# A residual sum moved from VectorE to TensorE and ScalarE, and two more buffers for scanned pairs, in the first state-space layer of a four-layer network

## The chip, the cores and the metric

The kernel runs on one core of one Trainium2 chip. A core has TensorE (matrix products, results into PSUM), VectorE, ScalarE and GpSimd for work on tiles, and a sync engine that issues most of the DMAs. The profile calls them PE (with PEld for the weight loads), DVE, ACT, POOL and SP. Each engine takes its instructions in the order in which the program lists them, and waits on semaphores for the others. The metric is the time of one execution on the device in microseconds (us), the median of several runs.

## The reference, cut to what matters

The input is `x` of 8 samples, 384 channels, 32 x 32 pixels, all in fp32. Four layers follow each other, each with a residual: `x = x + layer(group_norm(x))`. Layer 0 is a state-space layer (Mamba), layer 1 a deformable convolution, layer 2 a second state-space layer with a layer norm and an MLP, layer 3 a shift with a small convolution. The change touches layer 0 alone, where the 1024 pixels of a sample are a sequence:

```python
xz = xseq @ in_proj_w.T                 # 384 -> 2 x 768 channels
xin, z = jnp.split(xz, 2, axis=-1)
u = silu(causal_conv3(xin) + conv_b)
dt, Bm, Cm = split(u @ x_proj_w.T)      # 24, 16 and 16 wide
dt = softplus(dt @ dt_proj_w.T + dt_proj_b)
# for each token, 768 channels x 16 states:
h = exp(dt * A) * h + (dt * u) * Bm     # the scan
y = sum over the states of h * Cm, plus u * D
out = (y * silu(z)) @ out_proj_w.T      # 768 -> 384 channels
x = x + out                             # the residual
```

## The kernel before, in words

**Tiling.** In layer 0 a *step* is one half (512 tokens) of one sample, so there are 16 steps; even steps are first halves, odd ones second halves, which take the state over from the first. The 768 inner channels are 6 blocks `j` of 128 partitions, the 16 states are 8 pairs `m`. One *unit* is one `(j, m)`: a tile of 128 partitions x (2 states x 512 tokens). A step has 48 units, t = 0 to 47.

**One unit.** ScalarE writes the decays `da` into PSUM (`decays`, L437, two instructions, two buffers). GpSimd writes `db` (`inputs`, L442, three buffers). VectorE scans (`scan`, L452) and multiplies by C (`with_c`, L466) into a tile `hs`. In 3 or 4 units of every 16 GpSimd does that product instead (L463), and then the scan itself writes into `hs`. TensorE sums the pairs into the PSUM tile `y` by products with the identity (`read_out`, L483). The tiles `hs` have four buffers; one is free again when its two `read_out` products are done. A unit's `read_out` is put one to three units later than its scan. After the eight pairs of a block, VectorE multiplies `y` by the gate (`close`, L503, in slot 1, 9, 17, ... of the step); `y` has a single buffer.

**The order of everything else.** The engines' order is written out by hand. `plan` makes four lists of slots (`act`, `dve`, `pool`, `pe`), one slot per unit, and the loop over the units empties a slot of each as it goes. The slots hold work on three steps at once: the current one, the next one (`nxt`: norm, input projection `inner` L333 in slots 15, 16, 17, 24, 25, 26, convolution, `x_proj`, `dt_proj`) and the previous one (`prev`: its output projection). Within a unit `act` comes first, then the scan, `with_c`, `keep_last` (even steps: ScalarE saves the last state, L458), the decays of unit t + 2, then `dve`, `pool` and `pe`.

**The output projection.** `out_proj` (L516) sums, for each of three blocks `o` of output channels, six products `wout x u` of the previous step into a PSUM tile, three products in slot 8 and three in slot 9 (then 10 and 11, 12 and 13). `out_take` (L536, slots 11, 13 and 15 of `dve`) adds the tile to the residual tile `x` on VectorE and writes it there; after the third block one DMA stores it (L527). `x` was loaded by `residual` (L508). All PSUM tiles of projections share three buffers (tag `mm`), the `dt_proj` tile (L389, slots 6, 14, ...) among them. After the last step the three blocks follow each other without other work between them.

**Waits that matter below.** `soft_exp` (L395 to L398, `act`, slot 15 for one of the blocks) waits for `dt_proj` of slot 14; `conv_last` (L337, `act`, slot 16) waits for `inner` of slot 15; `close` in slot 17 waits for the `read_out` products of the eight pairs before it.

Of the kernel before, what the change touches and what calls it, by code (L numbers as in the profile page):

```python
# [8 lines left out]
F32 = mybir.dt.float32  # L9
AF = mybir.ActivationFunctionType  # L10
ALU = mybir.AluOpType
# [4 lines left out]
P = 128  # L16
# [6 lines left out]
ND = DI // P  # L23
# [3 lines left out]
TS = L // 2  # L27
# [64 lines left out]
class Net:  # L92
# [107 lines left out]
    def ssm_layer(self, li, src, dst, shift=None):  # L200
        tc, nc, ins = self.tc, self.nc, self.ins
        mlp = li == 2
        gp_c, gp_add = GP_C[li], GP_ADD[li]
        with ExitStack() as ctx:
            wp = ctx.enter_context(tc.tile_pool(name=f"w{li}", bufs=1))
            p1 = ctx.enter_context(tc.tile_pool(name=f"p1_{li}", bufs=1))
            p2 = ctx.enter_context(tc.tile_pool(name=f"p2_{li}", bufs=2))
# [5 lines left out]
            for h in (1, 0):  # L213
                x = p2.tile([P, G, TS], F32, name="x", tag="x")
# [44 lines left out]
            def w_mid(src, k):  # L259
                t = p2.tile([P, k, W_MID // k], F32, name="wm", tag="wm", bufs=3)  # L260
                n = src.shape[2]
                nc.sync.dma_start(out=t[:, :, :n], in_=src)
                return t
# [180 lines left out]
            def scan(s, j, m):  # L444
                if j == 0 and m == 0 and s["h"] == 0:
                    s["sib"]["st"] = p2.tile([P, ND, NS], F32, name="st")
                da, db = s["da", m], s["db", m]
                h = da
                if m in gp_c[s["h"]][j % 2]:
                    h = s["hs", m] = p2.tile([P, 2, TS], F32, name="hs", tag="hs", bufs=4)  # L450
                h1, da1, db1 = (t.rearrange("p i l -> p (i l)") for t in (h, da, db))
                nc.vector.tensor_tensor_scan(h1, da1, db1, 0.0, ALU.mult, ALU.add)  # L452
                s["h", m] = h
# [6 lines left out]
            def with_c(s, j, m):  # L460
                c = s["bc"][m][:, 1]
                if m in gp_c[s["h"]][j % 2]:
                    nc.gpsimd.tensor_tensor(s["hs", m], s["hs", m], c, ALU.mult)  # L463
                else:
                    hs = s["hs", m] = p2.tile([P, 2, TS], F32, name="hs", tag="hs", bufs=4)
                    nc.vector.tensor_tensor(hs, s["da", m], c, ALU.mult)  # L466

            def add_pair(s, j, m):
# [41 lines left out]
            def out_proj(s, o, k0, k1):  # L510
                if k0 == 0:
                    wo = w_mid(wout_d[:, :, o * P : (o + 1) * P], ND) if mlp else wout[:, :, o * P : (o + 1) * P]
                    s["out", o] = self.psum("ps_o"), wo
                ps, wo = s["out", o]
                for k in range(k0, k1):
                    nc.tensor.matmul(ps, wo[:, k, :P], s["u"][:, k, :], start=(k == 0), stop=(k == ND - 1))  # L516

            def store(s, o):
                if mlp:
# [9 lines left out]
            def out_take(s, o):  # L529
                if mlp:  # L530
                    if o == 0:
                        s["t"] = p2.tile([P, G, TS], F32, name="t", tag="xn", bufs=3)
                    nc.scalar.copy(s["t"][:, o, :], s["out", o][0])
                else:
                    xo = s["x"][:, o, :]
                    nc.vector.tensor_tensor(xo, xo, s["out", o][0], ALU.add)  # L536
                    store(s, o)

            def mlp_up(s, q, f):
# [51 lines left out]
            def plan(prev, s, nxt):  # L591
                act, dve, pool, pe = queues = [[[] for _ in range(T + NU)] for _ in range(4)]

                def put(q, t, fn, *args):
                    if not args or args[0]:
                        q[t].append((fn, *args))

                for j in range(ND):
                    t = NU * j
                    put(dve, t + 1, close, *((s, j - 1) if j else (prev, ND - 1)))  # L600
                    put(pe, (0, 9, 18, 27, 33, 41)[j], z_proj, s, j)
                    g = (3, 11, 20, 29, 35, 44)[j]
                    put(act, g, gate, s, j)
                    if j in (2, 3):
                        put(act, g, silu, nxt, 3 * (j - 2), 3 * (j - 1))
                    put(act, g, exp_ln)

                    n, k = (s, j + 2) if j + 2 < ND else (nxt, j + 2 - ND)
                    put(pe, t + 6, dt_proj, n, k)
                    put(act, t + 7, soft_exp, n, k)  # L610
                    put(dve, t + 8, soft_rest, n, k)
                    put(act, t + 9, soft_ln, n, k)
                    put(pool, t + 10, soft_sum, n, k)
                put(pe, 0, norm_load, nxt)
                if nxt and nxt["h"] == 0:
                    put(dve, 2, norm_stats, nxt, 0)
                    put(dve, 3, norm_stats, nxt, 1)
                    put(dve, 3, lambda n: n.update(gn_mv=self.gn_aggr(n["gn_st"])), nxt)
                    put(pe, 4, lambda n: n.update(gn_ps=self.gn_mean(n["gn_mv"])), nxt)
                    put(dve, 5, lambda n: n.update(gn_grp=self.gn_dev(n["gn_mv"], n["gn_ps"])), nxt)  # L620
                    put(act, 6, lambda n: n.update(gn_dm=self.gn_square(n["gn_grp"][1])), nxt)
                    put(pe, 6, lambda n: n.update(gn_ps=self.gn_mean2(n["gn_dm"])), nxt)
                    put(dve, 7, lambda n: n.update(gn_var=self.gn_sum(n["gn_grp"][0], n["gn_ps"])), nxt)
                    put(act, 8, lambda n: n.update(gn=self.gn_rstd(n["gn_grp"][0], n["gn_var"])), nxt)
                    put(act, 8, lambda n: n["sib"].update(gn=n["gn"]), nxt)
                put(act, 9, norm_apply, nxt)
                if mlp:
                    put(pe, 10, ln_mean, nxt)
                    put(dve, 11, ln_center, nxt)
                    put(act, 12, ln_square, nxt)  # L630
                    put(pe, 12, ln_var, nxt)
                    put(act, 13, ln_rstd, nxt)
                    put(dve, 13, ln_scale, nxt)
                    put(act, 14, ln_affine, nxt)
                for d, t in enumerate((15, 16, 17, 24, 25, 26)):
                    put(pe, t, inner, nxt, d)
                    put(act, t + 1, conv_last, nxt, d)
                    put(dve, t + 2, conv, nxt, d)
                put(pe, 30, x_proj, nxt, 0, ND // 2)
                put(pe, 31, x_proj, nxt, ND // 2, ND)  # L640
                put(act, 32, x_store, nxt)
                for m in range(NU):
                    put(pool, 41 + m, load_bc, nxt, m)
                put(act, 7 if mlp else 9, residual, prev)
                for o, (t, e) in enumerate(((1, 2), (3, 4), (5, 6)) if mlp else ((8, 9), (10, 11), (12, 13))):
                    put(pe, t, out_proj, prev, o, 0, ND // 2)
                    put(pe, e, out_proj, prev, o, ND // 2, ND)
                    put(act if mlp else dve, e + (1 if mlp else 2), out_take, prev, o)
                if mlp:
                    ups = ((7, 8, 11, 13), (22, 23, 28, 29), (37, 38, 39, 40))  # L650
                    downs = ((19, 20, 21), (34, 35, 36), (43, 44, 45))
                    for q, g in enumerate((17, 33, 42)):
                        for f, t in enumerate(ups[q]):
                            put(pe, t, mlp_up, prev, q, f)
                            put(act, t + 1, up_take, prev, q, f)
                        put(act, g, gelu, prev)
                        put(act, g, exp_ln)
                        for o, t in enumerate(downs[q]):
                            put(pe, t, mlp_down, prev, q, o)
                            put(dve, t + 2, down_take, prev, q, o)  # L660
                return queues
# [6 lines left out]
            with tc.manual_schedule(engines=ENGINES):  # L668
                s = steps[0]
# [34 lines left out]
                for i, (s, j, m) in enumerate(units):  # L704
                    c, t = divmod(i, T)
                    if t == 0:
# [6 lines left out]
                        act, dve, pool, pe = queues  # L713
                        over = [q[T:] for q in queues]
                    mine = m in gp_c[s["h"]][j % 2]
                    for r in early.pop(i, ()):
                        read_out(*units[r])
                    run(act[t])
                    scan(s, j, m)
                    if not mine:  # L720
                        with_c(s, j, m)
# [14 lines left out]
                    if mine:  # L736
                        with_c(s, j, m)
# [6 lines left out]
                    k = 3 if mine else 2 if m in gp_add else 1  # L744
# [12 lines left out]
                    stats = list(range(last))  # L757
                for o in range(G):
                    out_proj(s, o, 0, ND)
                    out_take(s, o)  # L760
                if mlp:
                    kernels_a()
# [1084 lines left out]
```

## Time and profile before

| what | value |
|---|---|
| time, median of 3 runs (lowest, highest) | 9474.54 us (9471.22, 9475.02) |
| the profiled execution: time, span | 9480.32 us, 9478.5 us |
| mean granted TensorE clock of that execution | 0.948 |
| layer 0 within the span | about 60 to 3041 us |
| its steps, from first scan to first scan | first 177.4 us; then even ones 182 to 183, odd ones 188 to 192 |
| a scan / a product with C on VectorE | 2290 / 1225 ns |
| the residual add L536, 48 times | 677 ns |

A line of instruction groups gives the source line, engine, operation and tiles (out<-in), then the count, the busy time, the mean of one, and the idle time of the engine just before. Each fp32 matrix product is recorded as two MATMUL instructions, called passes here; so the 16 x 3 x 6 = 288 products of `out_proj` show as 576. In a timeline a line is a run of like instructions: start, length, engine, source line, and in brackets the engine's idle time before it with what ended it.

### The profile page before, as it was taken

To read this page: it belongs to the slowest core of one execution; us is meant where nothing else is said; L and a number is where in the kernel's file an instruction comes from. 1 tells how busy PE (TensorE), PEld (TensorE's weight loads), DVE (VectorE), ACT (ScalarE), POOL (GpSimd) and SP (SyncE) were. 2 spreads that over 40 slices of the span, in tenths; PEclk is the share of its full clock that TensorE was granted. 3 is DMA by queue.
4 is the path that set the end of the run, shared out by engine and by line. 5 is a ranking of instruction groups with operands and counts; after the bars stand their busy time and mean duration, and the time that the engine had idled before them with its cause. 6 is when DMAs were issued, how large, how long until landed. Compare 5 with 4: busy or idle time off the path is not lost. (4 is left out here: it accounts for less than half of the span.)

```text
span 9478.5 us, 87409 instructions
## 1 busy us (share of the span) xinstructions
PE 8496.4 (90%) x27916; PEld 4511.6 (48%) x27916; DVE 8121.2 (86%) x8881; ACT 6479.3 (68%) x10147; POOL 5774.0 (61%) x3801
## 2 busy tenths in 40 slices
PE   7898888889887899999999997699999999999987
PEld 3333333333333677677777776244343443434333
DVE  7999999999997678778778777899999999999973
ACT  6666666666664677778778777667777777777750
POOL 7888888888887000000000000899999999999974
PEclk8999999999998999999999998799999999999998
DMA  2111211121111233333333333233232433333336
GB/s 92 68 56 46 85 53 53 50 85 56 49 68 51 77 80 88 90 83 84 93 79 88 89 83 87 92 100 95 91 94 87 121 112 96 93 91 90 120 102 127
DMA packets 566065, 791.98 MB, mean 84 GB/s; under 512 B 244243, under 2 KB 397235, under 8 KB 542041
## 3 DMA queue, kind: packets, MB, share of 16 engines
q1 hardware_dynamic: 503492, 775.85, 27.9%
q10 hardware_dynamic: 62100, 10.44, 0.7%
q8 instruction: 223, 3.65, 0.2%
q14 instruction: 250, 2.04, 0.1%
HBM read 716.49 MB, written 69.66 MB: 83 GB/s over the span
## 5 line engine op out<-in xcount | busy, mean ns | idle before, releaser
L442 POOL TENSOR_TENSOR db<-du,bc 128x1024 f32<-128x1024 f32 x1536 | 3611.1, 2356 | 419.0 <-DVE hs L452 230.7
L452 DVE TENSOR_TENSOR_SCAN da<-da,db 128x1024 f32<-128x1024 f32 x1272 | 2912.7, 2290 | 199.4 <-ACT da L437 145.4
L483 PE MATMUL y<-hs,ident 128*128 128x512 f32 x5184 | 2605.0, 638 | 376.2 <-DVE hs L466 233.8
L437 ACT ACTIVATE da<-dt,na 128x512 f32<-128x512 f32 x3072 | 2120.0, 691 | 911.1 <-DVE hs L466 679.9
L410 POOL TENSOR_TENSOR dt<-dt,sp_e 128x512 f32<-128x512 f32 x192 | 244.2, 1272 | 2932.1 <-DVE sp_e L402 2932.1
L483 PEld LDWEIGHTS y<-hs,ident 128*128 128x128 f32 x5184 | 1018.0, 203 | 1863.2 <-issue 1125.3
L1515 PE MATMUL wacc<-fsm,fxk 128*128 128x221 f32 (+34 forms) x10624 | 1657.1, 315 | 98.1 <-DVE fsm L1485 95.5
L1515 PEld LDWEIGHTS wacc<-fsm,fxk 128*128 128x128 f32 x10624 | 1570.1, 195 | 236.5 <-DVE fsm L1485 159.5
L466 DVE TENSOR_TENSOR hs<-da,bc 128x1024 f32<-128x1024 f32 x1272 | 1557.7, 1225 | 115.5 <-PE y L483 12.1
L1485 DVE TENSOR_TENSOR fsm<-fhy,fhx 128x170 f32<-128x170 f32 (+42 forms) x3216 | 1170.8, 428 | 346.2 <-PE wacc L1515 319.3
L1445 ACT ACTIVATE fhy<-fpyx,cell 128x416 f32<-128x416 f32 (+9 forms) x1280 | 645.5, 576 | 388.7 <-DVE fsm L1485 388.7
L1468 DVE TENSOR_TENSOR fxk<-fxt,fwk 128x1024 f32<-128x1024 f32 (+1 forms) x688 | 787.2, 1180 | 10.3 <-ACT fxt L1247 10.3
L452 DVE TENSOR_TENSOR_SCAN hs<-da,db 128x1024 f32<-128x1024 f32 x264 | 602.4, 2282 | 70.4 <-POOL db L430 29.4
L463 POOL TENSOR_TENSOR hs<-hs,bc 128x1024 f32<-128x1024 f32 x264 | 622.3, 2357 | 35.8 <-ACT st L458 35.3
L470 POOL TENSOR_TENSOR hs<-hs 128x512 f32<-128x512 f32 x480 | 609.5, 1270 | 3.5 <-DVE hs L466 3.5
L566 PE MATMUL ps_m<-hid,wm 128*128 128x512 f32 x1152 | 535.9, 610 | 29.7 <-ACT hid L559 24.2
L544 PE MATMUL ps_h<-t,wm 128*128 128x512 f32 x1152 | 539.1, 606 | 16.0 <-DVE x L573 15.8
L1450 ACT ACTIVATE fhy<-fhy,cols 128x1344 f32<-128x1344 f32 (+10 forms) x368 | 530.7, 1442 | 12.0
L458 ACT COPY st<-da 128x2 f32<-128x2 f32 x624 | 97.9, 157 | 505.4 <-DVE hs L466 503.9
L1156 PE MATMUL ps_off<-fxn,fow 128*98 128x465 f32 (+10 forms) x896 | 386.6, 579 | 0.0
L1432 ACT ACTIVATE fhx<-fpyx,cell 128x544 f32<-128x544 f32 (+8 forms) x640 | 380.0, 666 | 0.0
L566 PEld LDWEIGHTS ps_m<-hid,wm 128*128 128x128 f32 x1152 | 220.5, 194 | 329.8 <-issue 261.4
(203 smaller groups left out, 9870.2 us busy)
## 6 DMA issues: line engine op xcount, KB each, us to landing
bc<-bcd SPq DMA_DIRECT2D x256, 1024.0 KB
fpyx<-fposd SPq DMA_DIRECT2D x640, 256.0 KB
wm<-in_w SPq DMA_DIRECT2D x96, 768.0 KB
x<-x SPq DMA_DIRECT2D x71, 768.0 KB
winr<-in_win SPq DMA_DIRECT2D x192, 192.0 KB
x<-in_x SPq DMA_DIRECT2D x40, 768.0 KB
fpyx<-fposd SPq DMA_DIRECT2D x24, 1024.0 KB
wm<-in_wout SPq DMA_DIRECT2D x48, 384.0 KB
```

Of the source, the lines that this page charges most:

```text
L437: nc.scalar.activation(da[:, i, :], s["dt", j], AF.Exp, scale=na[:, j, n : n + 1])
L442: nc.gpsimd.tensor_tensor(db, du, s["bc"][m][:, 0], ALU.mult)
L452: nc.vector.tensor_tensor_scan(h1, da1, db1, 0.0, ALU.mult, ALU.add)
L463: nc.gpsimd.tensor_tensor(s["hs", m], s["hs", m], c, ALU.mult)
L466: nc.vector.tensor_tensor(hs, s["da", m], c, ALU.mult)
L470: nc.gpsimd.tensor_tensor(hs[:, 0, :], hs[:, 0, :], hs[:, 1, :], ALU.add)
L483: nc.tensor.matmul(s["y"], self.ident, s["hs", m][:, i, :], start=first and i == 0, stop=k == NU - 1 and i == n - 1,)
L566: nc.tensor.matmul(ps, s["w2"][:, f, o * P : (o + 1) * P], s["hid", q][:, f, :], start=(f == 0), stop=(f == 3))
L1445: nc.scalar.activation(hy[:, at : at + (yb - ya) * W], pyx[:, 0, ya * W : yb * W], AF.Abs, bias=bias)
L1468: nc.vector.tensor_tensor(t[:, :n], x, wk[:, j : j + 1, :].to_broadcast([P, n, P]), ALU.mult)
L1485: nc.vector.tensor_tensor(self.sub(sm, at, [(r * w, n), (w, r), (1, w)]), self.sub(hy, hy_at[by] + xa, [(r * W, n), (W, r), (1, w)]), self ...
L1515: nc.tensor.matmul(a[:, ya - 4 * o : yb - 4 * o, xa:xb], k, self.sub(sm, sm_at[by], [(w, yb - ya), (1, w)]), start=False, stop=False,)
```

## The change

`hs` gets six buffers in layer 0 (four in layer 2, as before). The residual is no longer added by VectorE: a seventh product, the identity times the residual tile, goes into the same PSUM sum (`add_residual`, in `pe` slots 10, 12 and 14; in slot 14 it stands behind `dt_proj`), and ScalarE copies the sum from PSUM to the tile `x`, in `act` slots 11, 13 and 15 (in slot 15 behind `soft_exp`). The stop flag of the sum moves to the added product. The same is done for the three blocks after the last step. Layer 2 keeps its order and its operations.

```diff
+        nhs = 4 if mlp else 6
...
-                    h = s["hs", m] = p2.tile([P, 2, TS], F32, name="hs", tag="hs", bufs=4)
+                    h = s["hs", m] = p2.tile([P, 2, TS], F32, name="hs", tag="hs", bufs=nhs)
...
-                    hs = s["hs", m] = p2.tile([P, 2, TS], F32, name="hs", tag="hs", bufs=4)
+                    hs = s["hs", m] = p2.tile([P, 2, TS], F32, name="hs", tag="hs", bufs=nhs)
...
                 for k in range(k0, k1):
-                    nc.tensor.matmul(ps, wo[:, k, :P], s["u"][:, k, :], start=(k == 0), stop=(k == ND - 1))
+                    nc.tensor.matmul(ps, wo[:, k, :P], s["u"][:, k, :], start=(k == 0), stop=mlp and k == ND - 1)
+
+            def add_residual(s, o):
+                nc.tensor.matmul(s["out", o][0], self.ident, s["x"][:, o, :], start=False, stop=True)
...
-                    xo = s["x"][:, o, :]
-                    nc.vector.tensor_tensor(xo, xo, s["out", o][0], ALU.add)
+                    nc.scalar.copy(s["x"][:, o, :], s["out", o][0])
                     store(s, o)
...
-                    put(act if mlp else dve, e + (1 if mlp else 2), out_take, prev, o)
+                    if not mlp:
+                        put(pe, e + 1, add_residual, prev, o)
+                    put(act, e + (1 if mlp else 2), out_take, prev, o)
...
                     out_proj(s, o, 0, ND)
+                    if not mlp:
+                        add_residual(s, o)
                     out_take(s, o)
```

## The prediction

> **What bounds the kernel now.** I read the page's busy times first, then the busy times of layer 0 and of a stretch inside one step (columns: stretch, length, then busy us and count on PE, PEld, DVE, ACT and POOL, the granted TensorE clock, DMA share, GB/s).
>
> ```profile
> PE 8496.4 (90%) x27916; PEld 4511.6 (48%) x27916; DVE 8121.2 (86%) x8881; ACT 6479.3 (68%) x10147; POOL 5774.0 (61%) x3801
> 60.00:3041.00 2981.00, 2580.68 (x5568) 1063.27 (x5568) 2738.92 (x1870) 1909.67 (x3228) 2610.97 (x1652) 0.93 0.17 59
> 1573.70:1634.00 60.30, 59.05 (x136) 25.45 (x135) 55.07 (x39) 43.22 (x79) 50.40 (x25) 0.99 0.12 39
> ```
>
> Over layer 0 VectorE is the busiest (2739 of 2981 us, 92%), and a reader who stopped here would take work off VectorE. The last line says otherwise for a third of step 8 (slots 6 to 21): TensorE is busy for 59.05 of 60.30 us at a clock of 0.99. VectorE's waits in layer 0, longest total first (total, times, longest):
>
> ```profile
> DVE da L452 <- ACT da L437: 75.3, 82, 1.5
> DVE hs L452 <- PE y L483: 26.3, 21, 3.4
> DVE x L536 <- PE ps_o L516: 16.5, 10, 4.5
> DVE u L503 <- PE y L483: 12.9, 15, 2.1
> DVE hs L466 <- PE y L483: 12.1, 8, 2.2
> ```
>
> Lines two and five are the four `hs` buffers: 38.4 us. Line four is `close` on TensorE's sums. To see which of these end last I took the timeline of step 8, TensorE first:
>
> ```profile
> 1584.42 5.31 PE L516 MATMUL ps_o<-u,wout 128*128 128x512 f32 x12
> ...
> 1593.87 2.74 PE L516 MATMUL ps_o<-u,wout 128*128 128x512 f32 x6
> 1596.44 1.88 PE L483 MATMUL y<-hs,ident 128*128 128x512 f32 x4
> 1598.16 2.74 PE L516 MATMUL ps_o<-u,wout 128*128 128x512 f32 x6
> ...
> 1605.12 1.12 PE L389 MATMUL ps_dt<-dbc,wdt 24*128 24x512 f32 x2
> 1606.17 3.70 PE L483 MATMUL y<-hs,ident 128*128 128x512 f32 x8
> 1609.71 2.74 PE L333 MATMUL ps_in<-xn,win 128*128 128x512 f32 x6
> 1612.28 3.60 PE L483 MATMUL y<-hs,ident 128*128 128x512 f32 x8
> ```
>
> No line carries a bracket: TensorE never waits here. Its list packs the previous step's output projection and the next step's input projection on top of the read-outs, so from slot 6 on it falls behind VectorE. Then VectorE and ScalarE in slots 15 to 17:
>
> ```profile
> 1606.25 0.68 DVE L536 TENSOR_TENSOR x<-x,ps_o 128x512 f32<-128x512 f32 x1
> 1608.29 2.29 DVE L452 TENSOR_TENSOR_SCAN hs<-da,db 128x1024 f32<-128x1024 f32 x1 [1.36 <-PE y L483]
> 1615.91 0.69 DVE L503 TENSOR_TENSOR u<-y,sz 128x512 f32<-128x512 f32 x1 [1.22 <-PE y L483]
> 1606.28 0.69 ACT L395 ACTIVATE dt<-ps_dt,vec 128x512 f32<-128x512 f32 x1 [1.73 <-PE ps_dt L389]
> ```
>
> The read-outs at 1612.28 end at 1615.88 and `close` starts at 1615.91. So a step has two regimes: from `close` in slot 17 to slot 6 of the next step VectorE sets the time, from slot 6 to that `close` TensorE does. The timelines of steps 1 to 14 repeat this: `close` in slot 17 waits 1.22 us for TensorE in every even step from 2 on and 0.33 us in every odd one, and TensorE has no wait over 0.2 us between slot 8 and slot 20 in any.
>
> [...] Here the trace decides: within the stretch the passes follow without a gap. [...] (the products stand in the list's order), so an added product delays all behind it. [...] the trace's pass takes 429 ns (12 passes from 1584.42 to 1589.57), [...] and the clock is granted at 0.99. So these passes won't get faster.
>
> **The change part by part.**
>
> *Three products more per step on TensorE.* The shape and weights are those of the L483 row. Six passes took 1593.87 to 1596.44, 2.57 us. The products go in at about 1587.2 (between the halves of the x12 run), before 1598.16 and after the `dt_proj` of 1605.12: all three before the read-outs that `close` awaits. TensorE has no gap there to hide them, so `close` in slot 17 moves by +2.57 us. Bounds: nothing, if there were slack; 16 early passes of the odd step 9 at a low clock took 8.82 us, 0.55 us each, so at worst 3.3 us. I take 2.57.
>
> *VectorE loses L536*, 3 x 0.68 = 2.03 us per step. In slots 11 to 15 this only makes VectorE arrive earlier at a `close` where it waits already: worth 0. Had TensorE slack, it would be worth 45 x 0.677 = 30.5 us.
>
> *Six buffers.* The 38.4 us of waits fall in slots 8, 12 and 16 but for a trace of them: inside the TensorE stretch. They vanish, and VectorE waits as much longer at `close` in slot 17. The stall goes there. Bounds: 38.4 us gained, or 0; I take 0.
>
> *ScalarE gets the copies.* The nearest row is layer 2's copy of the same shape from PSUM (L533), 586 ns. Queued behind them on ScalarE are `keep_last` and the decays of unit t + 2. Slot 11: with the gate's two table loads of 1.28 us before it, the decays come up to 0.6 us late; VectorE has the time. Slot 13: the copy waits for a product at about 1599.0, the decays for slot 15 end near 1602.3, and scan 15 began at 1602.72: just in time. Slot 15: `soft_exp` moves by two products, 1.71 us, the copy adds 0.61 with its issue, so the decays of unit 17 move by 2.32. Their scan moves by 1.7 in step 8, where they were ready 0.7 us early, and by 2.32 in odd steps. VectorE has 1.22 us to spare before `close` in even steps, in odd ones 0.33; with `close` itself at +2.57 both are covered. If they weren't, the price would be 0.6 us a copy.
>
> *After `close`*, ScalarE's convolution (L337, which waits 2.14 us for TensorE at 1612.48) is later by the same 2.57 us, and all behind it keeps its distance: nothing gives the time back before the step ends.
>
> *DMAs.* The residual load is issued at 13.3 us of an odd step and in the step before for an even one; TensorE needs it after 38 us. The store (L527) goes about 4 us later and delays the next norm load behind it on SP's queue from about 62 to 66 us of the step; its data is for the next step. The order on SP's and GpSimd's queues in the layer stays. All hidden.
>
> *The sum.* Steps 1 to 14: 14 x 2.57 = 36.0. Step 15 has no next step, but its scan 17 waits 0.68 us for decays held up by `dt_proj`: 2.3. After the last step three products stand in the open, less a copy that is 0.09 shorter than the add: 2.5. Together +40.8 us. The profiled execution's span of 9478.5 becomes 9519, its time of 9480.3 becomes 9521; the median shown is 5.8 us below that execution, so 9474.5 + 40.8 = 9515.
>
> **Rivals.** (A) *VectorE is the bound throughout* and the change does what its parts suggest: 30.5 + 38.4 + 3.1 (the L536 waits that are not in the end piece, 16.5 less 3 x 4.46) - 2.5 = 69.5 saved, 9405. For it: 92% busy, against 87% on TensorE. Against it: the `close` lines. It decides from the point where TensorE's stretch holds over 2.57 us of idle time; the stretch shown holds 1.25, most of it at its end. (B) *Half absorbed*: a longer stretch spends less of itself at the low clock; 136 passes at 429 ns are 58.3 us against 59.05 busy, so 0.7 us a step is there, 10 us in all, and with the idle end of the stretch 1.2 us more: up to 28 us back, 9487 to 9505. Against it: the low-clock passes are at the start, ahead of the change. (C) *ScalarE's copies reach the path*: the odd steps have only a quarter of a us between 2.32 and 2.57. If each copy costs its 0.59 us, 45 x 0.59 = 27 us more, 9542.
>
> **How the numbers follow.** My forecast 0.80 (own range 9505 to 9523: 10 us regained by the clock, or 0.15 us a product of extra waiting), A 0.07, B 0.06, C 0.07. The range runs from 9493, which takes in most of B, to 9525, which leaves out A and most of C, some 0.15. A measurement of this kernel tells about 0.2%, 19 us, from no change: faster 0.07, within it 0.06 (the lower part of B and of my case's doubts), slower 0.87.
>
> **What would show it.** The waits of L452 and L466 on the read-outs almost gone; scan 17 waiting for its decays, and `close` in slot 17 still waiting for TensorE, about 2.1 us in even steps (VectorE later by 1.7, TensorE by 2.57) and 0.6 us in odd ones; no gap on TensorE between slots 8 and 20, with L520's 96 passes inside; steps of 185 and 192 us; L536 gone without a gain. I would be wrong if `close` in slot 17 stopped waiting for TensorE, or if TensorE showed idle time ahead of it.

## The result, and the profile after

The changed kernel takes 9525.62 us, the median of five runs (9522.57 to 9526.96). The kernel before, run beside it, takes 9473.63 us (9468.93 to 9475.02). The ratio is 1.0054, with a 95% interval of 1.0042 to 1.0066: slower by 52 us, or 0.5%. The forecast of 9515 had the sign right and was 11 us too low; the range ended at 9525, 0.6 us short of the time.

| us | before | after | difference |
|---|---|---|---|
| median of the runs | 9473.63 | 9525.62 | +52.0 |
| profiled execution: time | 9480.32 | 9526.95 | +46.6 |
| profiled execution: span | 9478.5 | 9525.1 | +46.6 |
| first scan to last scan of layer 0 | 2952.0 | 2996.1 | +44.1 |
| last scan to the end of the last add or copy of layer 0 | 21.8 | 24.3 | +2.5 |
| the rest of the program | 6439.9 | 6440.0 | +0.1 |

All of the 46.6 us lie in layer 0 and its end piece. The profiled execution of before lies 6.7 us over the median of its runs, that of after 1.3 us over: this is why the medians differ by 5 us more than the profiles, and no trace can say where those 5 us are. Single executions scatter by that much: the rest of the program took between 6430 and 6441 us in the thirteen profiled executions of this document whose edits do not touch it (all but number 8).

The page's busy times of the changed kernel (share of the span, count of instructions):

```profile
PE 8549.0 (90%) x28012; PEld 4541.2 (48%) x28012; DVE 8093.2 (85%) x8833; ACT 6500.2 (68%) x10195; POOL 5771.0 (61%) x3801
```

TensorE has 96 passes more and 52.6 us more busy time, VectorE 48 instructions fewer and 28 us less: the work has moved as the diff says. The instructions on the tile `ps_o` (least, median and largest duration in ns, first and last start in us):

```profile
L520 PE MATMUL ps_o<-x,ident x96: 592/593/697, 287.9 to 3084.0; 128*128 128x512 f32 x96
...
L539 ACT COPY x<-ps_o x48: 575/585/587, 289.2 to 3084.6; 128x512 f32<-128x512 f32 x48
```

VectorE's waits in layer 0, in the same view as before (total, times, longest):

```profile
DVE da L453 <- ACT da L438: 131.1, 102, 4.5
DVE sp_e L403 <- ACT sp_w L399: 49.7, 15, 4.4
DVE u L504 <- PE y L484: 34.8, 21, 2.4
```

The 38.4 us on the `hs` buffers are gone but for 0.5 us, as is the add. In their place VectorE waits for the decays (131 us in place of 75) and at `close` (35 us in place of 13), and it is no earlier. Step 8 shows why. Its TensorE timeline in slots 9 to 17 (start, length, then the run of instructions):

```profile
1606.09 1.02 PE L520 MATMUL ps_o<-x,ident 128*128 128x512 f32 x2
1606.94 2.74 PE L517 MATMUL ps_o<-u,wout 128*128 128x512 f32 x6
...
1618.10 1.02 PE L520 MATMUL ps_o<-x,ident 128*128 128x512 f32 x2
...
1625.92 1.12 PE L390 MATMUL ps_dt<-dbc,wdt 24*128 24x512 f32 x2
1626.97 1.13 PE L520 MATMUL ps_o<-x,ident 128*128 128x512 f32 x2
1627.93 3.60 PE L484 MATMUL y<-hs,ident 128*128 128x512 f32 x8
1631.37 2.74 PE L334 MATMUL ps_in<-xn,win 128*128 128x512 f32 x6
```

The three products stand where the prediction put them. Not one line has a bracket: TensorE had no gap for them. From 1606.09 to the next run at 1606.94 the first one costs 0.85 us, and three cost 2.57. VectorE at the end of that stretch, slots 14 to 17:

```profile
1629.68 0.69 DVE L403 SCALAR_TENSOR_TENSOR sp_e<-sp_w,ps_dt 128x512 f32<-128x512 f32 x1 [2.10 <-ACT sp_w L399]
1631.59 2.30 DVE L453 TENSOR_TENSOR_SCAN da<-da,db 128x1024 f32<-128x1024 f32 x1 [1.22 <-ACT da L438]
1637.58 0.69 DVE L504 TENSOR_TENSOR u<-y,sz 128x512 f32<-128x512 f32 x1 [2.36 <-PE y L484]
```

VectorE is held up three times, and the last time is the one that counts: `close` waits 2.36 us for TensorE (1.22 before). Whatever VectorE gains ahead of 1637.58, it gives back there. The same stretch by windows, the kernel before first (stretch, length, busy us and count on PE, PEld, DVE, ACT and POOL, the granted clock, DMA share, GB/s):

```profile
1577.70:1616.00 38.30, 38.30 (x90) 16.60 (x89) 33.86 (x24) 25.19 (x48) 31.30 (x16) 1.00 0.19 62
```

```profile
1598.20:1637.70 39.50, 39.50 (x92) 17.16 (x91) 30.81 (x21) 26.47 (x49) 30.84 (x15) 1.00 0.19 60
```

TensorE is busy for the whole of both, at the full clock; VectorE falls from 33.9 to 30.8 us with no effect. (The first stretch starts a little further ahead of `close` than the second: the pieces compared below have exact ends.)

I then cut every step at two points, the first pass of the output projection in slot 8 and `close` of slot 17. Sums over layer 0, worked out from the starts in both traces (differences are taken before rounding):

| piece, us | before | after | difference | predicted |
|---|---|---|---|---|
| first scan to first output pass, 7 odd steps (1 to 13) | 271.1 | 279.8 | +8.7 | 0 |
| the same, 7 even steps (2 to 14) | 211.9 | 213.9 | +2.0 | 0 |
| first output pass to `close` of slot 17, steps 1 to 14 | 14 x 36.64 | 14 x 39.22 | +36.1 | +36.0 |
| that `close` to the next step, odd | 800.7 | 798.3 | -2.5 | 0 |
| the same, even | 808.6 | 806.8 | -1.8 | 0 |
| step 15 | 169.3 | 171.1 | +1.8 | +2.3 |
| step 0 | 177.4 | 177.2 | -0.3 | 0 |
| after the last scan | | | +2.5 | +2.5 |
| sum | | | +46.6 | +40.8 |

The middle piece is 36.64 us in every one of the 14 steps before and 39.22 in every one after. What the prediction has no term for is the first row: before its stretch even begins, an odd step of the changed kernel takes 1.2 us longer on average (38.73 to 39.98). Nothing that was edited lies there but the buffers of `hs`, and these are not the cause: with six buffers alone (number 1 below) the first row is 271.9 us, with the four buffers and the product (number 2) 279.0. What differs is the clock. Odd step 7, 18 to 36 us after its first scan, in three windows of 6 us; the kernel before:

```profile
1377.40:1383.40 6.00, 5.22 (x22) 3.32 (x22) 5.91 (x7) 1.57 (x3) 4.25 (x5) 0.72 0.00 0
1383.40:1389.40 6.00, 5.42 (x23) 3.71 (x23) 5.93 (x6) 3.54 (x8) 6.00 (x3) 0.78 0.00 0
1389.40:1395.40 6.00, 6.00 (x10) 2.43 (x9) 5.14 (x6) 5.59 (x13) 4.67 (x7) 0.64 0.00 0
```

and the changed kernel:

```profile
1391.90:1397.90 6.00, 5.20 (x20) 4.68 (x21) 5.97 (x7) 1.59 (x3) 4.26 (x5) 0.53 0.01 1
1397.90:1403.90 6.00, 6.00 (x13) 2.52 (x12) 5.93 (x6) 3.61 (x8) 6.00 (x3) 0.50 0.00 1
1403.90:1409.90 6.00, 6.00 (x16) 3.86 (x17) 5.21 (x6) 5.64 (x13) 4.77 (x7) 0.54 0.01 3
```

The eighth column is the granted clock: it recovers in part in the kernel before (0.72, 0.78, 0.64) and stays near one half in the changed one (0.53, 0.50, 0.54), through the very slots in which TensorE falls behind. The record of the clock in the two traces holds 0.5 and 1.0 only, and each of its entries but the last (331 before, 327 after) lasts a whole number of stretches of 3.413 us, called clock windows here. In five of the seven odd steps of the changed kernel (5 to 13) it stays at 0.5 from about 18.4 to 35.5 us of the step. In the kernel before it does so in step 1 alone; the other odd steps have shorter spells with a return to 1.0 between them, or one from 20.4 to 34.1 (step 9). By odd step the output projection starts at 40.71, 37.69, 38.31, 38.41, 39.31, 38.30, 38.41 us before, and at 38.33, 37.72 and then five times at about 40.75 after.

The traces also show what these starts go with: the place of the step's first scan within a clock window, counted from the switches in each execution's own clock record. These are the 49 odd steps 1 to 13 of the seven profiled executions in which norm and projections keep their slots (before, after, numbers 1 to 4 and 7):

| first scan, us into its clock window | odd steps | output projection starts at, us of the step |
|---|---|---|
| 0.01 to 0.18 | 11 | 39.3 (one 38.3) |
| 0.42 to 0.52 | 7 | 38.3 |
| 0.96 to 1.89 | 7 | 37.6 to 37.7 |
| 1.98 to 2.58 | 17 | 40.5 to 40.8 |
| 2.60 and 2.80 | 2 | 42.2 and 36.7 |
| 3.24 to 3.40 | 5 | 38.3 to 38.4 |

From step 5 on, an odd step of the changed kernel and the even step behind it take 378.9 us together, which is 111.0 windows. So each odd step begins at the same place, 1.98 to 2.10 us into a window, and meets the long spell again. In the kernel before the pairs take 371.2 to 374.6 us, 108.8 to 109.7 windows, and the place moves from step to step.

### The profile page after: what moved, and what is told of

Same layout as the page of the kernel before. It is cut to its first block, busy times and chain, and to the rows that moved or that the text cites. A ratio compares the mean times of both kernels' runs of the same rounds, so it can differ in the third digit from the quotient of the medians.

```text
span 9525.1 us, 87505 instructions
## 1 busy us (share of the span) xinstructions
PE 8549.0 (90%) x28012; PEld 4541.2 (48%) x28012; DVE 8093.2 (85%) x8833; ACT 6500.2 (68%) x10195; POOL 5771.0 (61%) x3801
## 5 line engine op out<-in xcount | busy, mean ns | idle before, releaser
L1475 DVE TENSOR_TENSOR fxk<-fxt,fwk 128x1024 f32<-128x1024 f32 (+1 forms) x688 | 787.9, 1182 | 10.2 <-ACT fxt L1254 10.2
```

What stands on the lines that cost most here:

```text
L1475: nc.vector.tensor_tensor(t[:, :n], x, wk[:, j : j + 1, :].to_broadcast([P, n, P]), ALU.mult)
```

## The experiments

Each time is the median of 4 to 20 runs, beside the kernel before on the same chip; ratios are against that. "Stretch" is the piece from the first output pass to `close` of slot 17 (36.64 us before, 39.22 after).

### 1. Six buffers alone, on the kernel before

```diff
-    ... name="hs", tag="hs", bufs=4)
+    ... name="hs", tag="hs", bufs=4 if mlp else 6)     # in scan and in with_c
```

> The kernel before with six buffers for hs in layer 0 and nothing else. If TensorE sets the time from slot 6 to the close in slot 17 (my theory): the waits of the scan and of the product with C on TensorE go from 38 us to under 2, the close in slot 17 waits that much longer, and the time stays: 9474, within 6 us. If VectorE is the bound throughout (rival A): about 38 us less, 9435.

9471.29 us against 9474.02: ratio 0.9999 (0.9991 to 1.0008). The stretch is 36.64 us, as before. VectorE's waits in layer 0:

```profile
DVE da L452 <- ACT da L437: 95.3, 96, 1.5
DVE x L536 <- PE ps_o L516: 32.2, 17, 4.5
DVE sp_e L402 <- ACT sp_w L398: 17.7, 8, 2.5
DVE u L503 <- PE y L483: 16.3, 21, 2.1
```

The waits on `hs` for TensorE are gone and have gone to the decays (75.3 to 95.3), the add (16.5 to 32.2) and `soft_exp`'s chain (8.9 to 17.7). They have not gone to `close` in slot 17, as I had expected: it waits 0.40 us in odd steps (0.33 before) and mostly 0.33 in even ones (1.22 before). VectorE arrives earlier at places where it then waits. This is the first half of rival A, and it falls. Outside of the stretch the buffers are worth a little: from that `close` to the next step the odd steps take 2.3 us less in sum and the even ones 2.1, which is too little to show in the median.

### 2. The residual moved, with four buffers

```diff
-        nhs = 4 if mlp else 6
+        nhs = 4
```

> The changed kernel with four buffers for hs, so the residual's move alone. My theory: as the changed kernel, 9525 within 6 us, because the buffers only choose where VectorE waits; close in slot 17 about 39.2 us after the first pass of the output projection, as in the changed kernel (36.6 before). If the deeper buffers are what costs (rival): nearer to 9474 than to 9525. If VectorE is the bound: about 28 us under the kernel before, 9446.

9525.86 us, ratio 1.0056 (1.0039 to 1.0073): the changed kernel's time, with a stretch of 39.22. Here VectorE waits for buffers more than ever:

```profile
DVE hs L453 <- PE y L484: 77.9, 28, 4.7
DVE hs L467 <- PE y L484: 19.4, 7, 3.5
```

That is 97 us of buffer waits, and taking them away (the changed kernel) gains nothing. The buffers only choose where VectorE waits for TensorE.

### 3. The product kept, the copies on VectorE

```diff
-    nc.scalar.copy(s["x"][:, o, :], s["out", o][0])
+    nc.vector.tensor_copy(s["x"][:, o, :], s["out", o][0])
...
-    put(act, e + (1 if mlp else 2), out_take, prev, o)
+    put(act if mlp else dve, e + (1 if mlp else 2), out_take, prev, o)
```

> The changed kernel, but VectorE copies the sum from PSUM in the slots where it used to add; ScalarE has no copy. My theory: the three products alone carry the cost, so 9525 within 6 us. If ScalarE's copies are the cost (rival C): 27 us less, about 9498, and the wait of scan 15 and scan 17 for their decays gone with it.

9527.1 us, ratio 1.0058 (1.0041 to 1.0075), stretch 39.22. The copies have moved, at 691 ns in place of ScalarE's 585:

```profile
L539 DVE COPY x<-ps_o x48: 680/691/693, 292.0 to 3084.6; 128x512 f32<-128x512 f32 x48
```

ScalarE without the copies is worth nothing, and `close` in slot 17 waits for TensorE with either engine's copies (2.51 us in even and 0.79 in odd steps here, 2.36 and 0.70 in the changed kernel). So they cost nothing in the changed kernel, and rival C, 27 us for them, falls.

### 4. All but the product

```diff
-    ... start=(k == 0), stop=mlp and k == ND - 1)
+    ... start=(k == 0), stop=k == ND - 1)
...
-    put(pe, e + 1, add_residual, prev, o)     # and the call after the last step
```

> The changed kernel without the identity product: the residual of layer 0 is left out of the result; ScalarE copies, hs has six buffers, VectorE has no add. My theory: the time of the kernel before, 9474 within 6 us, though VectorE has 32 us less to do; 36.6 us from the first pass of the output projection to the close in slot 17. If VectorE is the bound (rival A): 9404. If ScalarE's copies cost: 9500.

9472.7 us against 9474.02: ratio 0.9998 (0.9989 to 1.0007), stretch 36.7 on average. VectorE has lost its add, ScalarE has the copies, `hs` has six buffers, and the time is that of the kernel before. The residual of layer 0 is missing from the result. So the 52 us are the product's alone, and 32 us of work taken off VectorE are worth nothing. In even steps `close` in slot 17 waits 1.50 us for TensorE. In odd steps it waits for nothing, and the stretch is 36.72 us: there VectorE comes last by 0.08 us, after waiting 6.13 us for `soft_exp`'s chain on ScalarE. So for odd steps this run shows that VectorE's own work is not the limit, but not that TensorE is the last at `close`.

### 5 and 6. The output projection six slots earlier, without the product and with it

If the step's stretch is bound by TensorE because three jobs are packed into it, moving one of them to slots 2 to 7 should gain. Number 5 starts from number 1, number 6 from the changed kernel:

```diff
-    put(act, 7 if mlp else 9, residual, prev)
-    for o, (t, e) in enumerate(((1, 2), (3, 4), (5, 6)) if mlp else ((8, 9), (10, 11), (12, 13))):
+    put(act, 7 if mlp else 3, residual, prev)
+    for o, (t, e) in enumerate(((1, 2), (3, 4), (5, 6)) if mlp else ((2, 3), (4, 5), (6, 7))):
```

> The kernel before with six buffers for hs, and the output projection of the previous step put into slots 2 to 7 in place of 8 to 13 (the residual's load into slot 3), where TensorE has idle time. VectorE adds the residual as before. My theory: 36 passes, 15.4 us a step, leave the stretch that the close in slot 17 ends; what they find in idle time in front, some 6 to 9 us, is gained up to the point where VectorE becomes the bound, its waits before slot 18 being 4 to 6 us a step: 9400 to 9430. If TensorE's queue was not the bound: 9474 within 6 us. If the three PSUM buffers that the projections share are too few in slots 4 to 7: slower than 9474.

> The changed kernel (identity product, ScalarE copies, six buffers) with the output projection in slots 2 to 7 as in the run before it. My theory: where TensorE has room, taking the add off VectorE pays, so this is the faster of the two, by up to 2.0 us a step, 30 us. If TensorE stays the bound also with the early order: slower than the run before it by 2.57 us a step, 36 us.

Number 5 takes 9469.98 us, ratio 0.9995 (0.9987 to 1.0004): the expected gain of 45 us or more is missing. Even steps take 181.6 us, some 0.7 less; odd ones take 187.8 to 192.6. TensorE and VectorE in step 7 of number 5:

```profile
1375.76 5.47 PE L516 MATMUL ps_o<-u,wout 128*128 128x512 f32 x6
```

```profile
1404.68 0.69 DVE L503 TENSOR_TENSOR u<-y,sz 128x512 f32<-128x512 f32 x1 [8.40 <-PE y L483]
```

In odd steps the work has been moved into the very slots that run at half clock: six passes take 5.47 us where they take 2.74 elsewhere, and now `close` in slot 9 waits 5.5 to 8.4 us. The bound has only moved from one `close` to another. In even steps (8, 10 and 12) VectorE no longer waits for TensorE ahead of `close` in slot 17, but it still waits 5.3 us there, mostly for decays from ScalarE (5.6 to 5.9 us before, of which 2.2 to 2.6 for TensorE); the expected gain had taken all of these waits as gone. The third expectation, too few PSUM buffers, falls: TensorE waits only 1.8 us in all of layer 0 for a buffer that VectorE still holds (`ps_o` on `gn_var`). Number 6 takes 9478.54 us, ratio 1.0005 (0.9996 to 1.0014): 47 us under the changed kernel and 8.6 over number 5. Its `close` waits 70 us in layer 0 all told, 2.17 in slot 9 of an even step and 6 to 8 of an odd one. So a fixed price of 36 us for the product is wrong as well: the price depends on what else stands in its stretch.

### 7. The product issued twice

```diff
     def add_residual(s, o):
+        nc.tensor.matmul(s["out", o][0], self.ident, s["x"][:, o, :], start=False, stop=False)
         nc.tensor.matmul(s["out", o][0], self.ident, s["x"][:, o, :], start=False, stop=True)
```

> The changed kernel with the identity product issued twice, so the residual of layer 0 is added twice. A dose: my theory says another 2.57 us in each of 14 steps, 2.3 to 2.6 in step 15 and at the end: 41 us on top of the changed kernel's 9525, so 9566 within 8, and 41.8 us from the first pass of the output projection to the close in slot 17. If only the first three products hit a limit by chance of phase: less than 20 on top.

9557.65 us, ratio 1.0088 (1.0071 to 1.0105): 32 us over the changed kernel where I expected 41. The two products and `close` of step 8:

```profile
1622.46 1.02 PE L520 MATMUL ps_o<-x,ident 128*128 128x512 f32 x2
1623.31 1.02 PE L521 MATMUL ps_o<-x,ident 128*128 128x512 f32 x2
```

```profile
1656.52 0.69 DVE L504 TENSOR_TENSOR u<-y,sz 128x512 f32<-128x512 f32 x1 [3.22 <-PE y L484]
```

The second product costs what the first does (1622.46 to 1623.31, 0.85 us), and the stretch is 41.79 us, 2.57 more once again. The miss is in the other piece: odd starts fall back to 38.51 us on average, 10.2 less in sum than in the changed kernel, while even ones add 4.1. The term that made the change dearer than its products made this one cheaper. It does not go by the amount of work: from step 5 on a pair of steps takes 382.3 us here, 112.0 windows, and the odd steps begin 0.45 to 0.52 us into a window, the place of the 38.3 us starts in the table above.

### 8. The group norm's little products one slot later

In each of the five long spells of the changed kernel the recorded clock falls to 0.5 while TensorE waits 2.72 us for the norm of the next sample, 0.3 to 0.4 us before the end of that wait (in step 7 at 1392.31 us; the norm's first pass starts at 1392.70). Moving that chain shifts the waits, on the changed kernel. The edit acts in layer 2 as well, which has the same chain:

```diff
-    put(pe, 4, lambda n: n.update(gn_ps=self.gn_mean(n["gn_mv"])), nxt)
+    put(pe, 5, lambda n: n.update(gn_ps=self.gn_mean(n["gn_mv"])), nxt)
...
# likewise: gn_dev 5 to 6, gn_square 6 to 7, gn_mean2 6 to 7, gn_sum 7 to 8, gn_rstd 8 to 9
```

> The changed kernel with the group norm's chain for the next sample one slot later (its first products in slot 5 in place of 4, and so on). It tests where the 11 us beyond my sum come from. In odd steps of the changed kernel TensorE waits 2.7 us for the norm in slot 4 and then runs at half its clock until slot 8, and the output projection begins at 40.7 us of the step, against 38.7 on average before. If that wait causes the slow spell: the projection begins at 38 to 39 us in odd steps and the time is 9510 to 9518. If the spell is only a matter of how the step falls against the clock's periods: starts that scatter between 37.6 and 42.2, and a time within 8 us of 9525.

9521.45 us, ratio 1.0049 (1.0033 to 1.0066). Windows of step 7 at the same places of the step as above:

```profile
1391.90:1397.90 6.00, 4.56 (x24) 2.64 (x22) 5.96 (x8) 2.09 (x4) 4.27 (x4) 0.86 0.00 1
1397.90:1403.90 6.00, 5.02 (x7) 2.22 (x8) 5.88 (x6) 3.24 (x7) 6.00 (x4) 0.57 0.00 0
1403.90:1409.90 6.00, 4.19 (x24) 2.72 (x23) 5.97 (x6) 5.27 (x10) 5.63 (x7) 1.00 0.01 3
```

The clock now recovers within the spell (0.86, 0.57, 1.00), and three odd starts drop to 37.56 us; but two are at 39.26 and two at 40.9, so the sum is 273.0 (279.8 in the changed kernel, 271.1 before). The spell can be broken up, but this place of the norm doesn't do it in all steps. Here too the start goes with the place in the window, by a table of its own: 37.56 us for first scans at 1.86 to 2.08 us, 39.26 at 2.13 and 2.40, 40.9 at 1.37 and 1.51. That fits the second of the two expectations. In layer 0 this run is 6.3 us faster than the changed kernel, first scan to last; the program behind it takes 4.3 us longer in this profile.

### 9 to 11. The input projection later

The other job in the stretch is the next step's input projection. Number 9 puts it past `close` of slot 17, on top of number 1; number 10 does it on the changed kernel, number 11 on the kernel before with its four buffers.

```diff
-    if j in (2, 3):
-        put(act, g, silu, nxt, 3 * (j - 2), 3 * (j - 1))
+    if j in ((2, 3) if mlp else (3, 4)):
+        h = j - (2 if mlp else 3)
+        put(act, g, silu, nxt, 3 * h, 3 * (h + 1))
...
-    for d, t in enumerate((15, 16, 17, 24, 25, 26)):
+    for d, t in enumerate((15, 16, 17, 24, 25, 26) if mlp else (22, 23, 24, 30, 31, 32)):
...
# x_proj from slots 30 and 31 to 35 and 36, x_store from 32 to 37
```

> The kernel before with six buffers for hs, and the input projection of the next step in slots 22, 23, 24, 30, 31, 32 in place of 15, 16, 17, 24, 25, 26, with its activation, x_proj and store moved behind it. This takes 6 passes from in front of the close in slot 17 and 12 from just behind it, and puts them where TensorE waits for VectorE, without touching the slots before 9. My theory: the close in slot 17 comes at least 2.6 us earlier in the step, VectorE is the bound from there, and the time falls by 2.6 to 4.5 us in 14 steps: 9410 to 9438. If the close in slot 17 is not what sets the step: 9474 within 6 us.

> The changed kernel with the same late input projection. Its close in slot 17 has 6 passes more in front of it than the run before, which has VectorE's adds in exchange. My theory: if TensorE still ends last before that close, 2.57 us a step slower than the run before it, 36 us; if VectorE ends last there, up to 2.0 us a step faster, 28 us. Since moving the 6 passes of the input projection just undoes the 6 passes of the identity product, I expect this one near the kernel before, 9465 to 9485.

> The kernel before with the late input projection and four buffers for hs. It tells whether the two buffers more are worth anything once TensorE is less pressed: with VectorE as the bound before slot 17, the waits on hs count in full, 20 to 38 us slower than with six; with TensorE still ending last there, no difference beyond 6 us.

| number | time | ratio (95%) | stretch, mean |
|---|---|---|---|
| 9: six buffers, add on VectorE | 9450.75 | 0.9976 (0.9967 to 0.9985) | 36.02 |
| 10: the changed kernel | 9485.25 | 1.0010 (1.0003 to 1.0017) | 37.63 |
| 11: four buffers, add on VectorE | 9454.46 | 0.9981 (0.9973 to 0.9989) | 35.78 |

Number 9 gains 23 us where 36 to 64 were expected. VectorE in odd step 7 of number 9, slots 11 to 17:

```profile
1401.09 0.69 DVE L536 TENSOR_TENSOR x<-x,ps_o 128x512 f32<-128x512 f32 x1 [1.82 <-PE ps_o L516]
...
1415.05 0.69 DVE L402 SCALAR_TENSOR_TENSOR sp_e<-sp_w,ps_dt 128x512 f32<-128x512 f32 x1 [2.48 <-ACT sp_w L398]
...
1419.88 0.68 DVE L503 TENSOR_TENSOR u<-y,sz 128x512 f32<-128x512 f32 x1
```

`close` no longer waits for TensorE, but VectorE had waited there for only 0.33 to 1.22 us, and now it waits ahead of `close` for what else comes late from TensorE: the projection's sum and `dt_proj`, through ScalarE. So two ends lay close to each other, and only the difference was to be had. Number 11 is 3.7 us over number 9, where 20 to 38 us were expected with VectorE as the bound: the buffers are worth little even here. With the product (number 10) the time is 34.5 us over number 9, and `close` is out of the list of VectorE's longest waits; at its head stand the decays and `soft_exp`'s chain:

```profile
DVE da L453 <- ACT da L438: 119.7, 93, 4.5
DVE sp_e L403 <- ACT sp_w L399: 51.6, 15, 4.4
```

The second is ScalarE's work behind the `dt_proj` product of slot 14, which stands behind three blocks of the output projection. The first, 4.5 us ahead of scan 15 in every odd step, is the copy of slot 13: it stands ahead of the decays on ScalarE and waits for its product, here in step 7:

```profile
1415.35 0.58 ACT L539 COPY x<-ps_o 128x512 f32<-128x512 f32 x1 [8.07 <-PE ps_o L520]
```

So the price of the new order is still paid, though TensorE no longer ends last at `close`: it comes through ScalarE, where the copy holds up what stands behind it by its wait, not by its own 0.58 us. The copies were not moved back to VectorE here, so how the 34.5 us divide between them and the products is not shown.

### 12. Late input projection, and the output projection spread out

On number 10, with the second block one slot later and the third past `close` of slot 17, so that nothing of the third block stands ahead of `dt_proj` and of that `close`:

```diff
-    for o, (t, e) in enumerate(((1, 2), (3, 4), (5, 6)) if mlp else ((8, 9), (10, 11), (12, 13))):
+    for o, (t, e) in enumerate(((1, 2), (3, 4), (5, 6)) if mlp else ((8, 9), (11, 12), (18, 19))):
```

> The changed kernel with the late input projection (slots 22, 23, 24, 30, 31, 32) and the three blocks of the output projection spread over slots 8 and 9, 11 and 12, 18 and 19, their identity products and copies one and two slots behind. In front of the close in slot 17 stand 14 passes less than in the run with the late input projection alone, so TensorE should no longer end last there, and the add that VectorE no longer has, 2.0 us a step, should count. My theory: 20 to 30 us under the run with the late input projection and VectorE's adds (9450.75), so 9420 to 9432, the fastest of all. If taking the add off VectorE is worth nothing even then: 9445 to 9455. If the later output projection only moves the jam to the close in slot 25: above 9460.

9421.89 us over five runs (9415.65 to 9424.09) against 9475.69: ratio 0.9940 (0.9926 to 0.9953). It is the fastest of all: 54 us under the kernel before, 104 under the changed one, 63 under number 10. VectorE's waits in slots 0 to 17 of step 8 and the stretch up to `close`, by windows:

```profile
DVE da L453 <- ACT da L438: 5.0, 4, 1.5
```

```profile
1552.10:1586.90 34.80, 34.80 (x81) 15.03 (x80) 30.81 (x21) 24.65 (x44) 32.07 (x16) 1.00 0.07 23
```

VectorE has one kind of wait left there, and none on TensorE or on `soft_exp`. TensorE has 81 passes in the stretch where the changed kernel has 92. The stretch is 33.65 us on average; even steps take 179.0 to 179.3 us and odd ones 183.7 to 187.7, with output projections that start anywhere from 36.65 to 40.74 us. The same spreading with the add on VectorE wasn't tried, so this run shows what the place of the work is worth, not that the product is better than the add.

## Why the prediction was right and wrong

- **What bounds the kernel: right.** TensorE ends last from slot 6 to `close` in slot 17: that `close` waits for it in each of the steps 1 to 14, before and after. Number 4 frees VectorE of 32 us and gains nothing; number 7 adds 2.57 us to TensorE and the stretch is 2.57 us longer. In odd steps the lead is small: without the products (number 4) VectorE, held up by ScalarE, ends last by 0.08 us.
- **The products, 14 x 2.57 = 36.0 us: right to a tenth**, in the piece for which it was worked out (36.64 to 39.22 us in every step).
- **VectorE's add at 0 and the buffers at 0: right within the stretch** (numbers 4, 1 and 2). The stall went to `close` in slot 17, as said: 2.36 us in even steps and 0.70 in odd ones, predicted 2.1 and 0.6. Part of it went to the decays and to `soft_exp`, ahead of that `close`; in number 1 almost all of it did, which the prediction had not foreseen.
- **ScalarE's copies at 0: right in the sum, wrong in the walk.** The step "slot 13 just in time" was walked through in an even step. In odd steps it is not in time: the copy waits 8.07 us for its product at the head of ScalarE's list, scan 15 behind it waits 4.5 us for its decays, and VectorE waits 4.4 us for `soft_exp`'s chain. The price of 0.6 us a copy in case they weren't covered left this wait out. That the copies cost nothing still holds here (number 3), since TensorE reaches `close` later than VectorE does.
- **Everything before the stretch and after `close` at 0: wrong, and this is the step that failed.** The sum was made of the added products' durations alone and took the start of the stretch to stay where it was, 38 us into an odd step. It moved by +8.7 us over the odd steps and +2.0 over the even ones, together with longer spells of TensorE at half clock (in an even step two windows on end from about 19 us, where five of seven had one before), while the rest of the step gave back 4.3, much as it does with six buffers alone (4.4, number 1). I had seen the low clock at the start of odd steps and used it with the wrong sign: the lower end of my own range and rival B had the clock give time back, an estimate that no trace showed. A term of either sign was called for, of some 10 us (in numbers 7 and 8 the odd starts are 10 and 7 us lower in sum than in the changed kernel). Which sign it takes could not be told from the profile of before: the starts go with a step's place in a clock window of 3.413 us, and so with the length of a pair of steps (108.8 to 109.7 windows before, 111.0 after).
- **Step 15 and the end:** 1.8 and 2.5 us, predicted 2.3 and 2.5: right but for half a microsecond.
- **From the profile to the median:** the profiled execution was taken to lie 5.8 us over the median after the change too; it lies 1.3 over. With the 46.6 us of the profiles the forecast would have been 9521; the last 4.5 us are not explained by any view, and are within the scatter of single executions.
- **Steps of 185 and 192 us:** even ones 184.9 to 185.5; odd ones 191.6, 191.0 and then 194.0. It is the later odd steps that hold the missing term.

The five long spells in a row of the changed kernel go with its pairs of 111.0 windows, which bring each odd step to the same place. What stays open is why the pairs settle on a whole number of windows (111.0 here, 109.0 in number 4, 112.0 in number 7), and no run shifts a step's place alone, with all else left as it is.

## What to carry to other kernels

Cut a repeating step at the points where one engine waits for another, and ask for each piece which engine ends last; work taken off the engine that is busiest over the whole was worth nothing here in a piece where another ends last (32 us of it in number 4, ratio 0.9998), and deeper buffers there only moved the stall (97 us of buffer waits in number 2, for the same time as without them). An addition to the engine that ends last cost its full length here (2.57 us a step, twice), so make room in the piece first, and look at the end that lies next behind it: number 9 gained only 23 us because VectorE had been ready at most 1.22 us ahead of TensorE, and number 12 gained 54 by thinning out all that stood ahead of both. Work handed to an engine with slack held up what stood behind it in that engine's list while it waited for its input (8.07 us for a copy of 0.58). Where the granted clock changes within a step, leave a term of either sign for the parts of the step that weren't touched, and compare the step's new length with the clock's windows (3.413 us here).

## What the runs showed of the hardware that was not expected

- Six passes of 512 columns took 5.47 us in the half-clock spell of an odd step (number 5) and 2.74 elsewhere, and in the changed kernel the spell was as long as 17.1 us, five windows of 3.41, although TensorE was recorded as busy for most of it (6.00 of 6.00 us in two of the windows shown, at clock 0.50 and 0.54). So a TensorE that looked full did not have its full clock here. In step 7 the norm's 36 passes over one or two columns, 0.21 us apart, fill 7.7 of the 17.1 us and are recorded as busy; the last of the five windows is the only one in which none of them starts, and the clock was back after it. No run tests whether they are the cause.
- The start of the output projection in an odd step goes with the place of the step's first scan in a clock window (46 of the 49 odd steps of the table fall into five groups about 0.3 us wide or less), and in the changed kernel a pair of steps lasts a whole number of windows (378.9 us, 111.0 of 3.413), so that the same place comes back every time.
- The start of otherwise equal odd steps scattered by up to 3 us in one execution (37.69 to 40.71 before, 37.56 to 40.9 in number 8), though the stretch after it repeats to a hundredth of a microsecond in each of these runs.
